# Idle TensorE turns, score vectors as rows, averages by chunk, and other due times in a two-layer graph kernel

## The chip, the cores and the metric

The kernel runs on one core of a Trainium2 chip. The metric is the device time of one execution in microseconds (us). TensorE (PE) multiplies and turns (transposes) tiles, VectorE (DVE), ScalarE (ACT) and GpSimd (POOL) work on elements, and SyncE (SP) issues most of the transfers; ACT and POOL issue the others. Each engine works through its own instructions in order and waits for others by semaphores.

## The reference

There are B = 32 graphs of N = 512 nodes with D = 128 features, and one adjacency matrix for all of them. Layer 0 is a graph attention, layer 1 a gated recurrence of five steps; both are added to their input.

```python
# layer 0
h = max(layernorm(x), 0) @ W
logits = leaky_relu(h @ a_src [:, None] + h @ a_dst [None, :], 0.2)
out = softmax(logits where adj > 0) @ h + b
x = x + leaky_relu(out, 0.3)
# layer 1, input h = max(layernorm(x), 0), five times:
m = adj @ h                      # in and out matrix are both adj
u3 = h @ u3_w.T + u3_b
z = sigmoid([m, m] @ w3_w.T + w3_b + u3)
r = sigmoid([m, m] @ w4_w.T + w4_b + u3)
hv = tanh([m, m] @ w5_w.T + w5_b + (r * h) @ u5_w.T + u5_b)
h = (1 - z) * h + z * hv
# result: x + h
```

## The kernel before, in words

Each graph is a tile of 128 partitions by K = 4 rows of 128 features. The program is not written in the order in which it runs. It adds tasks: each has an engine, its columns (from which `COST` gives a duration), a key (its due time, lower is earlier), what it needs, and the buffers or PSUM banks that it takes. `plan` (lines 69 to 121) then plays the engines forward: whichever engine can begin first takes the task with the lowest key among those that may begin about then. The tasks are issued in that order and `pin` keeps it. So a change of a key or of a price changes the order on every engine from there on, though no instruction.

What is done once, at the start: SP loads x of the first three graphs, the adjacency `a_sb` (1 MB), the weights and biases (`load_rest`); ACT's queue loads W (`gw`) and both score vectors, each spread over all 128 partitions (`across`, line 386). DVE multiplies `gw` with each (line 422), summing along the row, which gives `wa` = W a_src and W a_dst; ACT writes these beside W into `wrow` (430 to 433), so that one product `hp` (line 714) gives h and its scores. The adjacency is turned in blocks by TensorE (`at_ps`, line 449, four groups of four) and copied by ACT into `adjT` (457).

Layer 0 of a graph (`layer0`): layer norm (statistics at 570, 576, 577; the power on POOL at 582; for graph 0 centre and scale on DVE at 587 and 591, else ACT at 606); a turn of h (the first `DIRECT` = 4 graphs by TensorE, `t_a`, line 623; later ones by a DVE block transpose and transfers through DRAM on POOL's queue); the product hp; exponentials and scaling on ACT (`hw`, 720 and 725); the scores spread over partitions (`es`, line 739, four turns for the first four graphs, transfers after that); four weight tiles `pt` on DVE (784), one for each chunk c of 128 neighbours; and the average `av` on TensorE (809), two parts with two halves each, over all four chunks. DVE normalizes (819, 821), applies the leak (836), adds x (839), and a second layer norm gives hN, which is turned (`t_b`) into the state hT.

A step of `recurrence`: m from the two halves `hi` and `lo` of h (line 886, eight instructions), a copy mT (897), the gates g (905, 906, then 925), tanh on ACT (911, 932), rh on DVE (918), the candidate v (941, 942), its tanh (947), and three DVE operations (953, 959, 962) that update hT. Then h is turned back for the next step: for the first steps of the first `SHORT` graphs, and for the last step of the last `SHORT_END` = 3 graphs, by TensorE (`h`, line 977, four turns); otherwise by a DVE block transpose (990), one store and four loads on SP's queue (996, 1001). After the last step DVE adds x1 (1026) and SP stores the result (1031).

Due times: `due(b)` is 5 steps of 6100 ns for each graph, 3 in the last `LEVEL` = 8 graphs; a step of the recurrence is due `WIDTH` = 6 later than the one before; layer 0 begins `LEAD` = 11 steps ahead. In the last eight graphs the keys are capped so that all end together.

Of the kernel before, what the change touches and what calls it, by code (L numbers as in the profile page):

```python
# [10 lines left out]
F32 = mybir.dt.float32  # L11
F32R = mybir.dt.float32r
AF = mybir.ActivationFunctionType
ALU = mybir.AluOpType

P = 128
Q = 32
G = P // Q
STEPS = 5
# [3 lines left out]
PACE = 3  # L23
# [1 line left out]
SLOTS = 10  # L25
DIRECT = 4
SHORT = 3
SHORT_END = 3
LEVEL = 8
STEP = 6100  # L30
LEAD = 11
# [4 lines left out]
    "POOL": (650, 0, 130),  # L36
    "SP": (430, 0, 0),
}
LANDING = 2600

WAIT = {"DVE": 200, "ACT": 200}
# [231 lines left out]
def gat_then_gated_gnn_kernel(  # L273
# [20 lines left out]
    nc = tc.nc  # L294
    B, N, D = x.shape
    K = N // P
# [14 lines left out]
    pin = tc.keep_in_program_order  # L311
    tasks = []

    def add(*args, **kwargs):
        tasks.append(Task(*args, **kwargs))
        return tasks[-1]

    def new(buffer, name, shape=(P, N)):
        tag = buffer.tags[0]
        if "bank" in buffer.tags:  # L320
            buffer.tile = psum.tile([P, N], F32, tag="bank", name=name)
        elif tag in ("way", "turn", "line"):
            buffer.tile = dram.tile(list(shape), F32, tag=tag, name=name)
        else:
            buffer.tile = pools[BUFFERS[tag]].tile(list(shape), F32, tag=tag, name=name)
        return buffer.tile


    ident = const.tile([P, P], F32, name="ident")
    make_identity(nc, ident)  # L330
    ones = const.tile([P, P], F32, name="ones")
# [28 lines left out]
    prep = fast.enter_context(tc.tile_pool(name="prep", bufs=1))  # L360
    a_sb = prep.tile([P, K, N], F32, name="a_sb")
    gw = prep.tile([P, D], F32, name="gw")
    across = prep.tile([P, 2, D], F32, name="across")
    cols = prep.tile([P, 5], F32, name="cols")
    sums2 = prep.tile([P, 2], F32, name="sums2")
    half = const.tile([P, 2], F32, name="half")
# [16 lines left out]

    nc.scalar.dma_start(out=gw, in_=g_w)
    for i, v in enumerate((g_asrc, g_adst)):
        nc.scalar.dma_start(out=across[:, i, :], in_=v.partition_broadcast(P))

    def load_rest(name):
        if name == "a":
# [18 lines left out]
    bias_loaded = add("SP", [1] * 5, -9.4e9, lambda: load_rest("bias"), (rest_loaded,), lands=1000)  # L408


    soon = -100 * STEP

    def issue():
        pin(nc.gpsimd.tensor_copy(wrow[:, :D], gw))
        pin(nc.gpsimd.tensor_copy(wsrc[:, :D], gw))

    w_copied = add("POOL", [1], soon, issue, at=3600)
    products = prep.tile([P, 2, D], F32, name="products")

    def issue():  # L420
        for i in range(2):
            pin(nc.vector.scalar_tensor_tensor(
                products[:, i, :], gw, 1.0, across[:, i, :], ALU.mult, ALU.mult,
                accum_out=wa[:, i : i + 1],
            ))

    wa_made = add("DVE", [128] * 2, soon + 1, issue, at=5900)

    def issue():
        pin(nc.scalar.copy(wrow[:, D : D + 1], wa[:, 1:2]))  # L430
# [7 lines left out]
        at=60 * STEP)  # L438

    adjacency = []  # L440
# [32 lines left out]
    t = add("POOL", [1] * 3, 0, issue, (rest_loaded,))  # L473
# [9 lines left out]
    t = add("PE", [256] * 5, 0, issue, (t,), (f_ws, f_us))  # L483
# [56 lines left out]
    t = add("DVE", [1] * 4, late, issue, (*counted, wa_made))  # L540
# [7 lines left out]
    t = add("PE", [256], late, issue, (t,), (f_viol,))  # L548
# [117 lines left out]

    def due(b):

        early = B - LEVEL
        return 5 * b if b < early else 5 * early + PACE * (b - early)  # L670

    def layer0(b):
        direct = b < DIRECT
# [5 lines left out]
        def keys(i):  # L679
            return begin + length * (base[0] + i) / parts  # L680

        f_x, loaded = xs.pop(b) if b in xs else load_x(b)
        f_h, f_hT, f_hw = Buffer("h0"), Buffer("h0T"), Buffer("hw")
# [7 lines left out]
        t = relu_layernorm(h, lambda: f_x.tile, f"a{b}", keys, (loaded,), (f_x, f_h), b == 0)  # L691
        base[0] = 5
        turn = transposed if direct else blockwise
        t = turn(hT, h, f"a{b}", keys, (t,), (f_h, f_hT))
# [5 lines left out]
        def hw():  # L700
            return f_hw.tile or new(f_hw, f"hw_{b}", (P, K, D + 3))
# [31 lines left out]
        if direct:  # L733
# [9 lines left out]
            t = add("PE", [256] * K, keys(0), spread, made, (f_hw, f_es))  # L743
        else:
# [9 lines left out]
            t = add("DVE", [64], keys(0), gather, made, (f_hw, f_lines))  # L754
# [23 lines left out]
            t = add("POOL", [1], keys(2), spread, stores, (way, f_es), lands=LANDING + 1500)  # L778
        base[0] = 15
        f_pts = [Buffer(f"pt{c}") for c in range(K)]  # L780
# [11 lines left out]
        weighed = [weigh(c) for c in range(K)]  # L792
# [3 lines left out]
        def o():  # L796
            return f_o.tile or new(f_o, f"o_{b}", (P, K, D))

        def average(part):
            f = Buffer("o", "bank")  # L800

            def avs():
                return f.tile[:, : 2 * (D + 1)].rearrange("p (c e) -> p c e", c=2)

            def multiply():
                new(f, f"av_{b}_{part}")
                for i in range(2):
                    for c in range(K):
                        pin(nc.tensor.matmul(  # L809
                            avs()[:, i, :],  # L810
                            lhsT=f_pts[c].tile[:, ts(2 * part + i, P)],
                            rhs=hw()[:, c, : D + 1],
                            start=(c == 0),
                            stop=(c == K - 1),
                        ))

            def normalize():
                rsum = pools[3].tile([P, 2], F32, tag="rsum", name=f"rsum_{b}_{part}")
                pin(nc.vector.reciprocal(rsum, avs()[:, :, D]))
                for i in range(2):  # L820
                    pin(nc.vector.scalar_tensor_tensor(
                        o()[:, 2 * part + i, :], avs()[:, i, :D], rsum[:, i : i + 1], bias0,
                        ALU.mult, ALU.add,
                    ))

            u = add("PE", [4 * (D + 1)] * 2 * K, keys(part), multiply, weighed,
                    (f, f_hw, *f_pts))
            return add("DVE", [40, 180, 180], keys(1 + part), normalize, (u, rest_loaded),
                       (f, f_o))

# [36 lines left out]
    def recurrence(b, step, halved, turned):  # L867

        key = (due(b) + WIDTH * step) * STEP
        if b >= B - LEVEL:  # L870
            key = min(key, (5 * B - LEVEL * (STEPS - 1 - step)) * STEP)

        def keys(i):
            return key + i * STEP / 4
# [4 lines left out]
        def aggregate(which, first):  # L879
            part = (his if first else los)[b % SLOTS]  # L880

            def issue():
                if first:
                    new(f_m, f"m_{b}_{step}")
                for k in range(K):
                    pin(nc.tensor.matmul(  # L886
                        f_m.tile, lhsT=part[:, k, :], rhs=adjT[:, k, :],
                        start=(first and k == 0), stop=(not first and k == K - 1),
                    ))

            return issue

        high, low = halved
        t = add("PE", [512] * K, keys(0), aggregate("hi", True), (high, *adjacency), (f_m,))
        t = add("PE", [512] * K, keys(0), aggregate("lo", False), (t, low), (f_m,))
        t_m = add("ACT", [480], keys(1),
                  lambda: pin(nc.scalar.copy(new(f_mT, f"mT_{b}_{step}"), f_m.tile)), (t,),  # L897
                  (f_m, f_mT))
# [68 lines left out]

        last = step == STEPS - 1
        nth = 5 * b + WIDTH * step
        if nth < 5 * SHORT or (last and b >= B - SHORT_END):  # L970

            f = Buffer("o", "bank")

            def turn():
                h_ps = new(f, f"h_{b}_{step}")
                for k in range(K):
                    pin(nc.tensor.transpose(h_ps[:, ts(k, P)], hT[:, ts(k, P)], ident))

            needs = (add("PE", [256] * K, keys(6), turn, (turned,), (f,)),)
            view = ("p k d -> p k d", {})  # L980

            def src():
                return f.tile.rearrange("p (k d) -> p k d", k=K)
        else:


            f_b, way, f = Buffer("blocks"), Buffer("way"), Buffer("rows")

            def blocks():
                pin(nc.vector.transpose(  # L990
                    new(f_b, f"blocks_{b}_{step}").rearrange("p (g k q) -> p g k q", g=G, k=K),
                    hT.rearrange("p (k g q) -> p g k q", g=G, k=K),
                ))

            def store():
                pin(nc.sync.dma_start(out=new(way, f"way_{b}_{step}"), in_=f_b.tile))

            def load(g):
                def issue():
                    rows = f.tile or new(f, f"rows_{b}_{step}", (P, G, N // G))  # L1000
                    pin(nc.sync.dma_start(
                        out=rows[ts(g, Q)],
                        in_=way.tile.rearrange("(a q) (g e) -> g q a e", a=G, g=G)[g],
                    ))

                return issue

            t = add("DVE", [512], keys(6), blocks, (turned,), (f_b,))
            t = add("SP", [1], keys(6), store, (t,), (f_b, way), lands=LANDING)
            needs = []  # L1010
            for g in range(G):
                needs.append(add("SP", [1], keys(6), load(g), (t, *needs[-1:]), (way, f),
                                 lands=LANDING))
            view = ("p k (a q) -> p a k q", {"a": G})

            def src():
                return f.tile.rearrange("p a (k q) -> p a k q", k=K)
# [69 lines left out]
```

## Time and profile before

| | us |
|---|---|
| median of three runs | 1169.24 (1169.11 to 1169.42) |
| the profiled execution | 1170.99 |
| its span | 1169.2 |
| TensorE waits for the adjacency at the start | 8.2 |
| first aggregation m begins | 29.20 |
| last product v of the recurrence begins | 1158.99 |

The table's last three rows are from the list of waits and the timeline. The span is the time from the first to the last instruction of the profiled execution. In the lines that follow, a group of instructions is told by its start, its duration, engine, line, operation, and output <- inputs; the bracket at the end is how long the engine had been idle and who ended that. In tables of stretches each engine has its busy time and its number of instructions; the three last columns are the clock granted to TensorE, the busy share of the DMA engines, and GB/s. Matrix products are pipelined: the busy time of a product includes its passage through the array, so that the distance between the starts of two that follow each other is the price of one.

### The profile page before, as it was taken

The page shows a single profiled execution, that of the slowest core. Times are in us where ns is not written, and L with a number is a line of the kernel's source. Part 1 is how long each engine was busy: PE and PEld are TensorE (multiplying, and loading weights), DVE is VectorE, ACT ScalarE, POOL GpSimd, SP SyncE. Part 2 cuts the span into 40 slices and gives each one's busy share as a digit, 9 for nine tenths or more (in the row PEclk, how much of TensorE's full clock was granted, in tenths as well). Part 3 has the DMA queues.
Part 4 walks back from the last instruction along what each step waited for, and adds up shares of the span by engine and source line. Part 5 has one row for each costly group of instructions (what it writes and reads, how often), then busy time and mean ns, then how long its engine had stood idle before and what let it go on. Part 6 is the DMA issues. An engine that isn't in the chain of part 4 may idle for free.

```text
span 1169.2 us, 14964 instructions
## 1 busy us (share of the span) xinstructions
PE 1145.9 (98%) x4267; PEld 701.6 (60%) x4267; DVE 947.4 (81%) x2120; ACT 649.8 (56%) x1263; POOL 347.7 (30%) x499
## 2 busy tenths in 40 slices
PE   6999999999999999999999999999999999999997
PEld 5665656555656556656655656656666566555553
DVE  5877988778998778988788888968989887667665
ACT  5655656465565565555565555566465554545543
POOL 2224433243442143332423344314254421100000
PEclk9999999999999999999999999999999999999998
DMA  3013344444445444443544444433454433332332
GB/s 109 21 43 100 111 137 124 124 125 122 133 119 137 126 143 129 125 131 113 141 130 129 119 122 147 136 115 109 129 146 128 128 111 117 98 98 74 106 109 78
DMA packets 137655, 135.62 MB, mean 116 GB/s; under 512 B 22496, under 2 KB 100960, under 8 KB 137440
## 3 DMA queue, kind: packets, MB, share of 16 engines
q1 hardware_dynamic: 119664, 97.64, 26.5%
q0 software_dynamic: 17472, 36.79, 12.5%
q8 instruction: 35, 0.57, 0.2%
q14 instruction: 52, 0.43, 0.1%
q10 hardware_dynamic: 432, 0.20, 0.1%
HBM read 71.83 MB, written 62.71 MB: 115 GB/s over the span
## 4 chain that ended last, share of the span: by engine, by line
PE 84%; DVE 2%; DMA 1%; ACT 1%; issue 0%; POOL 0%; SPq 0%; DVEq 0%; POOLq 0%
PE m L886 22%; PE g L925 11%; PE v L942 11%; PE v L941 10%; PE g L905 10%; PE g L906 10%; PE av L809 8%; PE hp L714 2%; DMA rows<-way 1%; DMA es<-line 0%; DVE hT L962 0%; DVE d L953 0%; DVE d L959 0%; ACT hv L947 0%; DVE pt L784 0%; DMA line<-lines 0%
## 5 line engine op out<-in xcount | busy, mean ns | idle before, releaser
L886 PE MATMUL m<-adjT,hi 128*128 128x512 f32 x640 | 196.4, 438 | 0.0
L886 PE MATMUL m<-adjT,lo 128*128 128x512 f32 x640 | 194.9, 436 | 0.0
L911 ACT ACTIVATE rs<-g,zrb 128x512 f32<-128x512 f32 x160 | 109.7, 686 | 146.2 <-PE g L906 145.9
L947 ACT ACTIVATE hv<-v,vb 128x512 f32<-128x512 f32 x160 | 109.8, 686 | 106.6 <-PE v L942 106.0
L953 DVE TENSOR_TENSOR d<-hv,hT 128x512 f32<-128x512 f32 x160 | 108.9, 681 | 72.9 <-ACT hv L947 72.2
L925 PE MATMUL g<-mT,w3dT 128*128 128x512 f32 x320 | 163.4, 594 | 1.5 <-ACT rs L911 1.5
L942 PE MATMUL v<-rh,u5hT 128*128 128x512 f32 x320 | 163.5, 592 | 1.2 <-DVE rh L918 1.2
L906 PE MATMUL g<-mT,w4sT 128*128 128x512 f32 x320 | 163.5, 592 | 0.0
L905 PE MATMUL g<-hT,u3T 128*128 128x512 f32 x320 | 163.5, 592 | 0.0
L941 PE MATMUL v<-mT,w5sT 128*128 128x512 f32 x320 | 163.4, 592 | 0.0
L897 ACT COPY mT<-m 128x512 f32<-128x512 f32 x160 | 93.8, 586 | 121.1 <-PE m L886 120.8
L932 ACT ACTIVATE zs<-g,zrb 128x512 f32<-128x512 f32 x160 | 109.6, 685 | 78.5 <-PE g L925 77.3
L886 PEld LDWEIGHTS m<-adjT,hi 128*128 128x128 f32 x640 | 119.2, 188 | 53.6 <-issue 29.4
L886 PEld LDWEIGHTS m<-adjT,lo 128*128 128x128 f32 x640 | 119.0, 188 | 50.6 <-issue 28.6
L918 DVE SCALAR_TENSOR_TENSOR rh<-rs,hT 128x512 f32<-128x512 f32 x160 | 109.0, 682 | 48.1 <-ACT rs L911 47.5
L809 PEld LDWEIGHTS av<-hw,pt 128*128 128x128 f32 x1024 | 123.1, 191 | 14.5 <-issue 10.3
L809 PE MATMUL av<-hw,pt 128*128 128x129 f32 x1024 | 123.8, 275 | 0.2 <-DVE pt L784 0.2
L962 DVE SCALAR_TENSOR_TENSOR hT<-d,hT 128x512 f32<-128x512 f32 x160 | 110.6, 691 | 13.6 <-PE v L942 0.5
L990 DVE STREAM_TRANSPOSE blocks<-hT 128x512 f32<-128x512 f32 x151 | 106.4, 707 | 10.6 <-DMA way<-blocks 6.4
L959 DVE SCALAR_TENSOR_TENSOR d<-zs,d 128x512 f32<-128x512 f32 x160 | 110.3, 690 | 4.6
L645 POOL DMA_DIRECT2D turn_b<-blocks_b x112 | 74.2, 665 | 118.0 <-DVE blocks_b L635 111.0
L942 PEld LDWEIGHTS v<-rh,u5hT 128*128 128x128 f32 x320 | 60.7, 190 | 78.1 <-issue 62.9
(112 smaller groups left out, 1360.4 us busy)
## 6 DMA issues: line engine op xcount, KB each, us to landing
way<-blocks SPq DMA_DIRECT2D x151, 256.0 KB, 2.1
rows<-way SPq DMA_DIRECT2D x604, 64.0 KB, 2.0
x<-in_x_dram SPq DMA_DIRECT2D x32, 256.0 KB, 2.9
out_dram<-res SPq DMA_DIRECT2D x32, 256.0 KB, 2.2
turn_a<-blocks_a POOLq DMA_DIRECT2D x112, 64.0 KB, 2.2
h0T<-turn_a POOLq DMA_DIRECT2D x28, 256.0 KB, 3.8
es<-line POOLq DMA_DIRECT2D x28, 256.0 KB, 3.8
turn_b<-blocks_b POOLq DMA_DIRECT2D x112, 64.0 KB, 2.2
```

The source lines that it names most:

```text
L809: pin(nc.tensor.matmul(avs()[:, i, :], lhsT=f_pts[c].tile[:, ts(2 * part + i, P)], rhs=hw()[:, c, : D + 1], start=(c == 0), stop=(c == K - 1),
L886: pin(nc.tensor.matmul(f_m.tile, lhsT=part[:, k, :], rhs=adjT[:, k, :], start=(first and k == 0), stop=(not first and k == K - 1),))
L905: pin(nc.tensor.matmul(g, lhsT=u3T, rhs=hT, start=True, stop=False))
L906: pin(nc.tensor.matmul(g, lhsT=w4sT, rhs=f_mT.tile, start=False, stop=True))
L911: pin(nc.scalar.activation(new(f_r, f"rs_{b}_{step}"), f_g.tile, AF.Tanh, bias=rb, scale=0.5))
L925: pin(nc.tensor.matmul(f_g.tile, lhsT=w3dT, rhs=f_mT.tile, start=False, stop=True, skip_group_check=True))
L932: pin(nc.scalar.activation(new(f_z, f"zs_{b}_{step}"), f_g.tile, AF.Tanh, bias=zb, scale=0.5))
L941: pin(nc.tensor.matmul(v, lhsT=w5sT, rhs=f_mT.tile, start=True, stop=False))
L942: pin(nc.tensor.matmul(v, lhsT=u5hT, rhs=f_rh.tile, start=False, stop=True))
L947: pin(nc.scalar.activation(new(f_hv, f"hv_{b}_{step}"), f_v.tile, AF.Tanh, bias=vb))
L959: pin(nc.vector.scalar_tensor_tensor(d, f_z.tile, 1.0, d, ALU.add, ALU.mult))
L962: pin(nc.vector.scalar_tensor_tensor(hT, f_d.tile, 0.5, hT, ALU.mult, ALU.add))
```

## The change

- `idle`: 56 tasks with the last key of all (1e12) turn the identity on TensorE into a bank of their own. The first 26 may begin at 0.7 us of the plan's time and are priced at 480 columns, the other 30 from 8 us at 256; the planner puts them wherever it sees TensorE free.
- The score vectors are loaded as two rows on one partition (`avecs`), and one product with a row of ones (`as_ps`) spreads them over the partitions in PSUM, from which DVE reads them.
- In the first four graphs the averages are four tasks for each part, one for each chunk, each needing only its own pt.
- The first `EARLY` = 6 graphs are due 4 steps apart, not 5, so all later due times come 6 steps earlier; the cap in the last eight moves with them.
- An m product is priced at 527 columns in place of 512; the instruction is the same.
- `SHORT_END` = 4, and the last two steps, not the last alone, are turned by TensorE in these graphs.

```diff
-SHORT_END = 3
+SHORT_END = 4
+EARLY = 6
...
+FIRST_IDLE, IDLE = 26, 30
...
-    across = prep.tile([P, 2, D], F32, name="across")
+    avecs = prep.tile([1, 2, D], F32, name="avecs")
...
-        nc.scalar.dma_start(out=across[:, i, :], in_=v.partition_broadcast(P))
+        nc.scalar.dma_start(out=avecs[:, i, :], in_=v.rearrange("(o d) -> o d", o=1))
...
+    f_idle = Buffer("o", "bank")
+
+    def idle():
+        pin(nc.tensor.transpose((f_idle.tile or new(f_idle, "idle"))[:, :P], ident, ident))
+
+    for i in range(FIRST_IDLE + IDLE):
+        add("PE", [480 if i < FIRST_IDLE else 256], 1e12, idle, (), (f_idle,),
+            at=700 if i < FIRST_IDLE else 8000)
...
+    f_as = Buffer("o", "bank")
+
+    def issue():
+        pin(nc.tensor.matmul(
+            new(f_as, "as_ps")[:, : 2 * D], lhsT=ones[0:1, :],
+            rhs=avecs.rearrange("o i d -> o (i d)"), start=True, stop=True,
+        ))
+
+    t = add("PE", [1024], soon, issue, (), (f_as,), at=4100)
...
-                products[:, i, :], gw, 1.0, across[:, i, :], ALU.mult, ALU.mult,
+                products[:, i, :], gw, 1.0, f_as.tile[:, ts(i, D)], ALU.mult, ALU.mult,
...
-    wa_made = add("DVE", [128] * 2, soon + 1, issue, at=5900)
+    wa_made = add("DVE", [150] * 2, -5.6 * STEP, issue, (t,), (f_as,))
...
     def due(b):
-        early = B - LEVEL
-        return 5 * b if b < early else 5 * early + PACE * (b - early)
+        at = since = 0
+        for until, pace in ((EARLY, 4), (B - LEVEL, 5), (B, PACE)):
+            at += pace * max(0, min(b, until) - since)
+            since = until
+        return at
...
+            def product(i, c, start):
+                pin(nc.tensor.matmul(
+                    avs()[:, i, :],
+                    lhsT=f_pts[c].tile[:, ts(2 * part + i, P)],
+                    rhs=hw()[:, c, : D + 1],
+                    start=start,
+                    stop=(c == K - 1),
+                    skip_group_check=True,
+                ))
...
+            def multiply_with(c):
+
+                def issue():
+                    if c == 0:
+                        new(f, f"av_{b}_{part}")
+                    for i in range(2):
+                        product(i, c, c == 0 and i == 0)
+
+                return issue
...
-            u = add("PE", [4 * (D + 1)] * 2 * K, keys(part), multiply, weighed,
-                    (f, f_hw, *f_pts))
+            if direct:
+                u = None
+                for c in range(K):
+                    u = add("PE", [4 * (D + 1)] * 2, keys(part), multiply_with(c),
+                            (weighed[c], u), (f, f_hw, f_pts[c]))
+            else:
+                u = add("PE", [4 * (D + 1)] * 2 * K, keys(part), multiply, weighed,
+                        (f, f_hw, *f_pts))
...
-            key = min(key, (5 * B - LEVEL * (STEPS - 1 - step)) * STEP)
+            key = min(key, (5 * B - EARLY - LEVEL * (STEPS - 1 - step)) * STEP)
...
-        t = add("PE", [512] * K, keys(0), aggregate("hi", True), (high, *adjacency), (f_m,))
-        t = add("PE", [512] * K, keys(0), aggregate("lo", False), (t, low), (f_m,))
+        t = add("PE", [527] * K, keys(0), aggregate("hi", True), (high, *adjacency), (f_m,))
+        t = add("PE", [527] * K, keys(0), aggregate("lo", False), (t, low), (f_m,))
...
-        if nth < 5 * SHORT or (last and b >= B - SHORT_END):
+        if nth < 5 * SHORT or (step >= STEPS - 2 and b >= B - SHORT_END):
```

On TensorE the new order begins with 17 idle turns, the product that spreads the vectors, nine more idle turns and the first adjacency turns; 30 idle turns stand among the work of the first three graphs, nine of them ahead of the first averages.

More of the change, by code (lines that the diff above doesn't have):

```diff
@@ L797, in o @@
             return f_o.tile or new(f_o, f"o_{b}", (P, K, D))
+        f_avs = [Buffer("o", "bank") for _ in range(2)]
         def average(part):
-            f = Buffer("o", "bank")
+            f = f_avs[part]
             def avs():
                 return f.tile[:, : 2 * (D + 1)].rearrange("p (c e) -> p c e", c=2)
+            def product(i, c, start):
[7 more added lines that the diff above has]
+                ))
             def multiply():
@@ L808, in multiply @@
                     for c in range(K):
[L809 to L815, printed above, removed]
+                        product(i, c, c == 0)
+            def multiply_with(c):
[5 more added lines that the diff above has]
+                return issue
             def normalize():
```

## The prediction

> **What bounds the kernel.** I read busy time first, then the chain of waits, then PE's own waits, then the stretches.
>
> ```profile
> PE 1145.9 (98%) x4267; PEld 701.6 (60%) x4267; DVE 947.4 (81%) x2120; ACT 649.8 (56%) x1263; POOL 347.7 (30%) x499
> ...
> PE 84%; DVE 2%; DMA 1%; ACT 1%; issue 0%; POOL 0%; SPq 0%; DVEq 0%; POOLq 0%
> ```
>
> TensorE is the bound. The time is its work plus the time in which it has none, and only three things can change: work, idle, and work done slowly. Where is it idle?
>
> ```profile
> 0.00:8.20 8.20, 0.00 (x0) 0.02 (x1) 2.10 (x13) 1.49 (x2) 2.64 (x9) 1.00 0.68 217
> 8.20:16.60 8.40, 7.19 (x32) 6.55 (x32) 4.40 (x26) 5.33 (x17) 4.17 (x9) 1.00 0.44 132
> 16.60:28.50 11.90, 9.71 (x69) 7.86 (x69) 9.25 (x26) 7.45 (x26) 1.39 (x1) 1.00 0.10 24
> 28.50:44.50 16.00, 15.49 (x95) 11.94 (x95) 15.10 (x54) 6.50 (x12) 3.03 (x3) 1.00 0.06 17
> 44.50:110.00 65.50, 65.50 (x280) 42.52 (x279) 48.26 (x122) 41.93 (x90) 24.02 (x34) 1.00 0.20 56
> 110.00:160.00 50.00, 48.31 (x182) 28.97 (x181) 44.23 (x110) 29.85 (x62) 22.64 (x32) 1.00 0.43 126
> 160.00:1130.00 970.00, 969.77 (x3525) 587.91 (x3524) 801.90 (x1741) 543.06 (x1033) 289.83 (x411) 1.00 0.42 122
> 1130.00:1160.00 30.00, 28.83 (x87) 15.09 (x85) 19.42 (x29) 13.51 (x21) 0.00 (x0) 1.00 0.31 101
> 1160.00:1169.20 9.20, 1.12 (x5) 0.71 (x4) 2.77 (x4) 0.69 (x1) 0.00 (x0) 0.65 0.17 62
> ```
>
> (The first busy column is PE.) From 44.5 to 1130 only 1.92 us are idle, so no edit there can give more. The rest is the head (8.2 without any work, then half-empty until 28.5) and the tail (1.17 in the last 30 us, then 9.2 after the last matrix product). The head is also slow:
>
> ```profile
> 9.17 0.29 DVE L422 SCALAR_TENSOR_TENSOR products<-gw,across 128x128 f32<-128x128 f32 x1 [0.50 <-DMA across<-in_L_gnn_a_dst_dram]
> ...
> 10.13 1.11 PE L623 MATMUL t_a<-ident,h 128*128 128x128 f32 x4 [0.81 <-DVE h L591]
> ...
> 15.35 0.87 PE L739 MATMUL es<-ident,hw 128*128 128x128 f32 x4
> ...
> 16.34 2.73 DVE L784 SCALAR_TENSOR_TENSOR pt<-es,hw,adjT 128x512 f32<-128x512 f32 x4 [2.21 <-PE es L739]
> ...
> 16.62 1.48 PE L623 MATMUL t_a<-ident,h 128*128 128x128 f32 x4 [0.41 <-ACT h L606]
> ...
> 19.12 3.17 PE L809 MATMUL av<-hw,pt 128*128 128x129 f32 x26 [0.17 <-DVE pt L784]
> ```
>
> Turns that follow each other start 0.22 us apart until 16.2 (the first four take 1.10, one of them 0.43) and 0.11 apart later (at 22.12, 22.23, 22.34), although the granted clock column says 1.00 throughout. So PE ran at half speed until between 16.2 and 16.6.
>
> **The change, part by part.**
>
> *Idle turns and score rows.* 26 turns of the identity stand ahead of the first adjacency turns, 30 more in gaps of the first graphs. At 0.22 us the 26 cost 5.7 us, from 1.35 (the identity is ready at 1.32) to about 7.1; the adjacency lands at 8.2, which hides them. After the 17th stands the product that spreads the score vectors; it waits for their DMA, with nine turns, the adjacency turns and everything else on PE behind it. The broadcast loads landed 7.0 and 7.5 us after issue; a row of 0.5 KB (the bias columns) took 2.5, gw 3.3. Landing thus lies between 4.2 and 9.2; I take about 5, as the row is nearest to the small loads. The two products on DVE (0.29 + 0.08 each) then end near 6.8 instead of 9.47, and the scale of h at 7.5 instead of 10.08.
>
> Whether turns raise the clock is the question. The row: at 11.04 to 16.2 PE ran turns, eight hp products (1.95 us) and turns again, and was fast by 16.6 (the next av starts are 0.11 apart). [...] my sum below would be about -0.4 us; by the trace, where more than half of the work before the rise was turns, it is -3.1. The trace can't exclude that the hp products alone did it. I take the trace. [...] here fast running came 6.1 to 6.5 us after work began at 10.13[...]. The new stretch of work is some 6 us long, so the rise should be there by 8.2, but not surely.
>
> *The first graph, replayed* in the new order on each engine with the durations of the rows (turn 0.11, hp 0.11, copy 0.59, hw 0.85 per half, pt 0.68), old end to new end: h scaled 10.08 to 7.5; t_a 11.24 to 9.3 (it stands behind the first adjacency turns, so behind 8.2); h0T copied 11.87 to 10.0; hp 14.69 to 11.1; es 16.21 to 12.7; last pt 19.07 to 15.6 (DVE must be through with two layer norms by 12.8; in the old order that work ended at 14.13, and it follows the landing of x).
>
> *Averages chunk by chunk.* Before, 26 of 32 av instructions ran after the last pt was begun, ending at 22.29. Now those of a chunk run beneath the next pt; 32 x 0.11 from 13.55 end at 17.2. Normalized at 18.4 instead of 23.14; hN scaled at 23.4 instead of 28.49; the first aggregation starts at 24.1 instead of 29.20. So 5.1 us are gained on graph 0.
>
> *What is late next: DVE.* From 23.4 the new order puts layer norms of graphs 3 and 4, a block transpose and graph 2's pts ahead of graph 1's normalization. Adding its rows (12 big ones of 0.7, eight pts, norms) gives graph 1's hN on ACT at 43.5 to 45.1; before, it ran at 41.67. PE would wait some 1.3 us there. Comparing what PE has then done: at 45.75 the new order has, beyond what the old had at 44.47, one m (1.85), one pair of g (1.72), hp (0.90), es and t_a (0.44 each), 5.35 us. The old one reaches this at 49.82. **Head: -4.1 us** (-1 to -5.6).
>
> *First six closer, later keys.* No instruction is added; all due times move by six steps together, so only the order in the ramp and chance order later change. `527` columns alters the planner alone (its price for an m product becomes 0.230, the row shows 0.231 between starts). Idle time in the middle was 1.92 us; the new order may have anything from 0 to about 7 (one step with a single graph in flight: at the end of this trace 10.2 us pass from the second half of m at 1152.73 to hT at 1162.90, and with the first half 0.93, turns 0.6 and cast 0.65 a step takes 12.4, against 1.85 + 5 x 0.86 = 6.2 of work). I take 1.9, the nearest row: **0 us**.
>
> *Last turns by TensorE.* Groups of four turns rise from 9 to 14, so five more. Each is 0.44 us of PE on the path: **+2.2 us**. Removed are five block transposes (0.71, DVE idle beside PE) and 25 DMA issues on SP, which lay beside PE. What they cost was waits in the tail:
>
> ```profile
> 1137.27 1.13 PE L925 MATMUL g<-mT,w3dT 128*128 128x512 f32 x2 [0.78 <-ACT rs L911]
> ...
> 1156.77 0.66 PE L977 MATMUL h<-ident,hT 128*128 128x128 f32 x4 [0.39 <-DVE hT L962]
> ...
> 1162.96 1.11 PE L977 MATMUL h<-ident,hT 128*128 128x128 f32 x4 [2.95 <-DVE hT L962]
> ```
>
> In the new order the last two graphs run interleaved to the end; between a graph's last product of step 3 and its turn stand 3.7 us or more of other work, where 3.0 are needed. Both waits go: **-1.2 us** (0 to -1.2). After the last product the chain (tanh, three DVE operations, turns, sum, store) stays 9.2 us. The last turns may be fast (PE idles 2.1 instead of 2.95 before them: -0.5), and two stores come together (+0.5): 0.
>
> **Sum:** -4.1 + 0 + 2.2 - 1.2 = -3.1 us. The profiled execution took 1170.99 with a span of 1169.2; 1.8 lie outside. The runs' median is 1169.24, so the forecast is **1166.1** (the profiled one about 1167.9).
>
> **Rivals.**
> 1. *The turns don't raise the clock.* For: [...] no stretch of turns alone was seen to end fast. Against: the mix at 11 to 16. Idle turns between hp and es then cost 0.22 each, es ends at 16.4 as before, and only the chunks save (av end 20.4 against 22.29). Head about -1.4: -1.4 + 2.2 - 1.2 = -0.4, **1168.8**, no change.
> 2. *DVE is not late.* The planner may order the ramp better than my rows say: head -5.1, no idle in the middle (-1.9): -6.0, **1163.2**. For: 65 us without idle in the old ramp. Against: DVE was busy 15.1 of 16.0 us at 28.5 to 44.5.
> 3. *Slower: recurrences starve PE in the ramp.* With DVE late for the second and third graph, at 45 to 110 us only graph 0 has steps to run; each such step costs 12.4 - 6.2 = 6.2 us. One such step brings +3.1 and decides from 5.4 us of new idle on (over 0.2% slower); one and a half give 9.3 - 3.1 = +6.2, **1175.4**, one alone **1172.3**, which I take. For: DVE load in the ramp. Against: the old ramp had the same work and no wait after 44.5.
>
> **How the numbers follow.** What a measurement can tell from no change is 0.2%, 2.3 us. Forecast case 0.46 (1163.5 to 1168), rival 1 0.22, rival 2 0.20, rival 3 0.12. Faster by over 2.3 us: most of the forecast case (0.40), rival 2 whole, a little of rival 1 (0.04): 0.64. Slower: rival 3 and a little of rival 1: 0.12. The rest, 0.24, is the same. The range reaches from rival 2's better side to rival 1's worse: 1162.0 to 1170.2.
>
> **What would show it.** Right: adjacency turns 0.11 us apart at 8.2; products on DVE over by 7; first m near 24; no idle of PE at 1130 to 1160; 56 turns for line 977's successor. Wrong: turns still 0.22 apart at 10 us; score rows landing after 7; PE idle above 5 us between 40 and 200.

## The result, and the profile after

| | before | after |
|---|---|---|
| median of 20 runs | 1169.54 (1168.44 to 1171.47) | 1167.82 (1165.95 to 1170.98) |
| profiled execution, its span | 1170.99, 1169.2 | 1165.95, 1164.1 |
| first m begins | 29.20 | 24.53 |
| last v begins | 1158.99 | 1153.03 |

The ratio is 0.9984 (95% interval 0.9978 to 0.9991): 1.7 us faster, inside the 0.2% that the prediction called no change. In a second comparison the same kernel gave 0.9992 (0.9984 to 1.0000). The two profiles are further apart, 5.0 us: the one of before lies 1.5 us above its median, the one of after is the fastest of its 20 runs. And the runs of the change spread over 5.0 us, those of before over 3.0. Why, is the question of the experiments.

Busy time first, from the page of the changed kernel:

```profile
PE 1151.7 (99%) x4345; PEld 708.7 (61%) x4345; DVE 942.9 (81%) x2115; ACT 647.8 (56%) x1263; POOL 347.8 (30%) x499
```

PE has 5.8 us more to do (idle turns and the tail's turns) and yet less time passes. The stretches (columns as before):

```profile
0.00:8.20 8.20, 5.82 (x31) 5.12 (x32) 3.32 (x19) 1.96 (x6) 2.64 (x9) 1.00 0.76 288
8.20:16.60 8.40, 8.40 (x74) 8.20 (x74) 5.54 (x24) 7.00 (x19) 4.17 (x9) 1.00 0.22 49
16.60:28.50 11.90, 11.40 (x88) 10.29 (x87) 11.22 (x43) 6.73 (x22) 1.90 (x2) 1.00 0.08 23
...
44.50:110.00 65.50, 65.18 (x298) 43.72 (x297) 53.74 (x151) 42.30 (x93) 29.12 (x41) 1.00 0.24 66
110.00:160.00 50.00, 50.00 (x180) 30.13 (x179) 46.84 (x106) 29.58 (x58) 22.93 (x34) 1.00 0.47 135
160.00:1130.00 970.00, 969.59 (x3514) 586.07 (x3513) 791.22 (x1711) 538.93 (x1025) 281.72 (x399) 1.00 0.41 120
```

From 44.5 to 1130 PE is idle for 0.73 us in place of 1.92. The start in the timeline, and the first m:

```profile
1.38 3.89 PE L418 MATMUL idle<-ident 128*128 128x128 f32 x17 [1.38 <-POOL ident masks.py:199]
...
6.27 0.67 PE L435 MATMUL as_ps<-avecs,ones 1*128 1x256 f32 x2 [1.00 <-DMA avecs<-in_L_gnn_a_dst_dram]
...
6.87 1.21 PE L418 MATMUL idle<-ident 128*128 128x128 f32 x9
...
7.91 0.65 PE L471 MATMUL at_ps<-ident,a_sb 128*128 128x128 f32 x4
...
13.34 3.84 PE L833 MATMUL av<-hw,pt 128*128 128x129 f32 x32
...
24.53 1.16 PE L933 MATMUL m<-adjT,hi 128*128 128x512 f32 x4
```

Take the passage of the last one, 0.43 or 0.27 us, from the duration and divide by the number of steps: the first 17 turns are 0.22 us apart, the nine 0.12. So in this execution PE was fast by 6.3, within 5 us of its first turn, where before it was fast from about 16 on. All 32 av now run in one piece beneath the pts.

The score rows did something that the prediction's sum did not have: the adjacency, loaded at the same time, comes earlier. Its line before and after (KB, then us from issue to landing):

```profile
a_sb<-in_adj_dram SPq DMA_DIRECT2D x1, 1024.0 KB, 6.9
...
a_sb<-in_adj_dram SPq DMA_DIRECT2D x1, 1024.0 KB, 5.1
```

Issued at 1.2, it is there at 6.3 in place of 8.1. All three traces with broadcast loads (before, before_pace4, across) have 6.9, the eleven with rows 5.1 or 5.2. At the end:

```profile
1153.03 1.02 PE L989 MATMUL v<-rh,u5hT 128*128 128x512 f32 x2
1154.52 0.63 PE L1024 MATMUL h<-ident,hT 128*128 128x128 f32 x4 [0.47 <-DVE hT L1009]
1157.08 0.66 PE L1024 MATMUL h<-ident,hT 128*128 128x128 f32 x4 [1.93 <-DVE hT L1009]
```

There are no waits between 1125 and the last v, and the last turns take 0.66 in place of 1.11. But from the start of that v to the end 11.07 us pass, where it was 10.21: two stores of 256 KB, issued 1.17 us apart at most, land 3.8 us (median) after issue; the one at the end of the kernel before took 3.1.

**Where the 5.0 us between the profiles came from.** The last v begins 5.96 earlier: five more groups of turns +2.2, idle time in the middle -1.2, in the tail -1.2, so the head gave 5.96 + 2.2 - 1.2 - 1.2 = 5.8 (by subtraction; 4.7 of it show at the first m). The end gives 0.86 back.

### The profile page after: what moved, and what is told of

Read it like the earlier page. It is cut to its first block, busy times and chain, and to the rows that moved or that the text cites. A ratio compares the mean times of both kernels' runs of the same rounds, so it can differ in the third digit from the quotient of the medians.

```text
span 1164.1 us, 15045 instructions
## 1 busy us (share of the span) xinstructions
PE 1151.7 (99%) x4345; PEld 708.7 (61%) x4345; DVE 942.9 (81%) x2115; ACT 647.8 (56%) x1263; POOL 347.8 (30%) x499
## 3 DMA queue, kind: packets, MB, share of 16 engines
q1 hardware_dynamic: 116064, 95.02, 25.8%
## 5 line engine op out<-in xcount | busy, mean ns | idle before, releaser
L933 PE MATMUL m<-adjT,hi 128*128 128x512 f32 x640 | 199.1, 441 | 0.3 <-ACT hi L910 0.3
L604 POOL TENSOR_TENSOR rs_b<-ve_b,mhalf 128x4 f32<-128x4 f32 x32 | 36.1, 1127 | 266.6 <-DVE ve_b L599 184.7
L1037 DVE STREAM_TRANSPOSE blocks<-hT 128x512 f32<-128x512 f32 x146 | 102.8, 707 | 9.6 <-DMA way<-blocks 7.2
```

Source lines behind the costliest of these rows:

```text
L933: pin(nc.tensor.matmul(f_m.tile, lhsT=part[:, k, :], rhs=adjT[:, k, :], start=(first and k == 0), stop=(not first and k == K - 1),))
```

## The experiments

Every ratio is to the kernel before on the same chip, with its 95% interval. The runs are from several chips, on which the kernel before had medians of 1169.05 to 1169.98, so differences of medians below 1 us between chips say little.

| run | median us | ratio |
|---|---|---|
| after_again (the change once more) | 1168.48 | 0.9992 (0.9984 to 1.0000) |
| no_idle | 1168.92 | 0.9995 (0.9987 to 1.0003) |
| tail_undone | 1165.44 | 0.9975 (0.9966 to 0.9984) |
| pace5 | 1173.80 | 1.0045 (1.0032 to 1.0058) |
| steady23 | 1166.01 | 0.9970 (0.9958 to 0.9982) |
| steady_tail | 1164.17 | 0.9953 (0.9939 to 0.9967) |
| across | 1169.69 | 1.0001 (0.9993 to 1.0010) |
| no_chunks | 1170.91 | 1.0010 (1.0003 to 1.0017) |
| before_pace4 | 1173.41 | 1.0031 (1.0019 to 1.0043) |
| price512 | 1165.56 | 0.9961 (0.9947 to 0.9975) |
| steady_first | 1166.13 | 0.9966 (0.9954 to 0.9978) |
| steady_tail_again | 1164.56 | 0.9959 (0.9945 to 0.9973) |

### The change once more: where its runs differ

> The changed kernel once more, for a second trace and the spread of its runs. Before the profile of the change lay 1.9 us below its median and that of the kernel before 1.5 us above its own, so the two profiles (5.0 us apart) say more than the medians (1.7 us). Theory A (the clock rises at a different moment in each run): the runs spread over 4 to 5 us again, median about 1167.8, and this trace, if it is a slower run, shows turns 0.22 us apart after 7 us. Theory B (the spread is made by transfers or by the end of the kernel): turns are 0.11 apart from 7 us on here too, and a slower trace differs at another place.

The runs spread from 1166.82 to 1170.65, and the profiled one was the slowest, with a span of 1168.9. The same order, in the timeline of this run:

```profile
1.38 3.89 PE L418 MATMUL idle<-ident 128*128 128x128 f32 x17 [1.38 <-POOL ident masks.py:199]
6.38 1.19 PE L435 MATMUL as_ps<-avecs,ones 1*128 1x256 f32 x2 [1.11 <-DMA avecs<-in_L_gnn_a_dst_dram]
7.50 2.18 PE L418 MATMUL idle<-ident 128*128 128x128 f32 x9
9.47 1.06 PE L471 MATMUL at_ps<-ident,a_sb 128*128 128x128 f32 x4
...
12.87 1.06 PE L739 MATMUL hp<-wrow,h0T 128*128 128x131 f32 x8
```

Here the nine turns are 0.22 us apart and so are the adjacency turns; only hp at 12.87 is fast. And since the nine turns stand ahead of the adjacency in PE's order, they push its turns to 9.47, though the adjacency had landed at about 6.4 (5.2 us after issue). The first m begins at 27.5 in place of 24.5: 3.0 of the 4.8 us between the two spans. Another 1.2 is a single wait of an av for its pt at 947.5. Theory A holds for the larger part. Of the five traces with the change's start, three were fast by 6.3 (the change, tail_undone, pace5) and two only at about 11 and 13 (no_chunks, this one).

**What the traces record of the clock.** Every trace keeps a list of the moments at which the clock granted to TensorE changed to 1.0 or to 0.5. The clock column is made from this list and counts the time ahead of the first entry as 1.00; after that entry it can be read. With the broadcast loads (run `across`, below) it gives:

```profile
6.06:9.48 3.42, 1.39 (x10) 0.96 (x8) 0.52 (x5) 0.00 (x0) 0.54 (x1) 1.00 0.95 321
9.48:16.30 6.82, 6.08 (x29) 6.08 (x30) 3.61 (x23) 4.72 (x15) 4.17 (x9) 0.50 0.35 83
```

Between two recorded changes lie 3.413 and then 6.827 us in this trace, 13.653 and 3.413 in `steady_first`, 1146.878 in the profile of before and 1153.705 in that of the change: 1, 2, 4, 1, 336 and 338 times 3.413 us. The first rise does not come at the same moment in two traces of the same start: at 5.54 in the change, at 12.85 in after_again. The table takes the 3.413 us ahead of a recorded change and, counted back from there (in before_pace4 forward), other stretches of that length; it gives the share of each in which PE ran turns or products:

| run | stretch, us | share | clock afterwards |
|---|---|---|---|
| the change | 2.13 to 5.54 | 0.92 | rises |
| pace5 | 2.57 to 5.98 | 0.79 | rises |
| after_again | 2.61 to 6.02 | 0.78 | stays at half |
| after_again | 6.02 to 9.43 | 0.57 | stays at half |
| after_again | 9.43 to 12.85 | 1.00 | rises |
| no_chunks | 0.67 to 4.09 | 0.79 | stays at half |
| steady_first | 4.03 to 7.44 | 0.74 | stays at half |
| steady_first | 7.44 to 10.86 | 0.90 | rises |
| across | 2.65 to 6.06 | 1.00, turns alone | rises |
| across | 6.06 to 9.48 | 0.41 | falls |
| steady_first | 21.10 to 24.51 | 0.47 | falls |
| before_pace4 | 146.20 to 149.61 | 0.48 | stays full |

The product as_ps, of a single row, is left out of these shares. With it the stretches 6.02 to 9.43 of after_again and 4.03 to 7.44 of steady_first would have 0.90 and 1.00, and the clock did not rise at their ends. In the rows above a rise followed shares of 0.79, 0.90, 0.92 and 1.00, and none followed 0.57, 0.74, 0.78 and another 0.79; the full clock fell after 0.41 and 0.47 and stayed after 0.48. What holds between and beyond these shares was not shown. What differs between the runs is how the same turns lie to such a stretch: the 17 (1.38 to 5.27) fill 0.92 of the one that ends at 5.54 in the change, and 0.78 of the one that ends at 6.02 in after_again.

### Without the idle turns

```diff
     def idle():
-        pin(nc.tensor.transpose((f_idle.tile or new(f_idle, "idle"))[:, :P], ident, ident))
+        pass
```

> The changed kernel in the same order, with the 56 idle turns not issued. If they raise the clock early: the first 24 turns and hp products from 8 us on are 0.22 us apart again, es ends 2.6 us later, and the kernel takes about 2.5 us more than the change (about 1170.3). If the gain of the head comes from the score rows and the chunks alone: at most 0.5 us more than the change, or less than the change, since nothing stands in PE's way.

It took 0.4 us more than the change on the same chip, which is the rival's number; but neither theory was right. The trace:

```profile
7.42 1.13 PE L471 MATMUL at_ps<-ident,a_sb 128*128 128x128 f32 x4
8.70 1.11 PE L645 MATMUL t_a<-ident,h 128*128 128x128 f32 x4
9.60 1.92 PE L471 MATMUL at_ps<-ident,a_sb 128*128 128x128 f32 x8
11.31 1.28 PE L739 MATMUL hp<-wrow,h0T 128*128 128x131 f32 x8
```

Turns are slow until the rise at 11.75, es runs 1.1 us later (12.90 in place of 11.81) and the first m begins at 25.7. That is 1.2 later than with idle turns in a good start, and 1.8 earlier than with them in a bad one. So the idle turns, as the change places them, win and lose: about nothing on average.

### The wait for the score rows taken out of the middle

```diff
-FIRST_IDLE, IDLE = 26, 30
+FIRST_IDLE, IDLE = 23, 30
...
-    t = add("PE", [1024], soon, issue, (), (f_as,), at=4100)
+    t = add("PE", [1024], soon, issue, (), (f_as,), at=5500)
```

PE's order is now 23 idle turns, the product that waits for the score rows, the adjacency turns. The question is whether the pause between turns and product (5.27 to 6.27 in the change) makes the spread of the runs.

> The change with 23 idle turns and then the product that waits for the score rows, directly ahead of the adjacency turns (17, product, 9 in the change); the order on the other engines is that of the change. [...] PE is busy from 1.4 to about 6.6 and again from 6.3 at the latest, so all or nearly all runs are fast by 8 us and the first m begins by 25 in the trace; median 1 to 2 us below the change, near its fastest runs (1166 to 1167), spread 3 us or less. If the spread has another cause: median within 0.5 us of the change and a spread of 4 us again.

The runs lie between 1165.16 and 1167.62, and the median of 1166.01 is at the change's fastest runs. The start of this kernel in the timeline:

```profile
1.38 5.16 PE L418 MATMUL idle<-ident 128*128 128x128 f32 x23 [1.38 <-POOL ident masks.py:199]
6.47 0.69 PE L435 MATMUL as_ps<-avecs,ones 1*128 1x256 f32 x2
7.09 0.75 PE L471 MATMUL at_ps<-ident,a_sb 128*128 128x128 f32 x4
```

The product begins without a wait (no bracket), and the adjacency turns follow at once. The pause alone does not decide it: in the change and in pace5 the clock rose at 5.54 and 5.98 within a pause of 1.0 us, after shares of 0.92 and 0.79. The 23 turns reach to 6.54, where the 17 end at 5.27. Of the five traces with this start four rose at 5.3 to 7.2; in the fifth (steady_first, below) the turns filled 0.78 of the stretch from 0.62 to 4.03, the next held the product, and the clock rose at 10.86. There the first m began at 25.8, not at 27.5, since no idle turn stands between the landing of the adjacency and its turns, and of these 1.3 us 0.5 come from a second fall of the clock. Both count: a late rise should be rarer (four of five traces against three of five would not show it alone, the narrower spread of the runs fits), and it costs less.

### Score vectors over all partitions again

```diff
-    avecs = prep.tile([1, 2, D], F32, name="avecs")
+    across = prep.tile([P, 2, D], F32, name="across")
...
-        nc.scalar.dma_start(out=avecs[:, i, :], in_=v.rearrange("(o d) -> o d", o=1))
+        nc.scalar.dma_start(out=across[:, i, :], in_=v.partition_broadcast(P))
```

The product as_ps is left out, and the two on DVE read `across`.

> The change with the score vectors loaded over all partitions again, without the product; 26 idle turns in one piece. The products on DVE then wait for the broadcast loads until 8.3 and 9.2, hp cannot begin before wrow at about 9.9, and h is scaled at 10.1 rather than 8.1; the adjacency turns go first. If the score rows' gain is on the path: first m 1.5 to 2 us later than in a good start of the change (26 to 26.5), median 1168 or more. If the wait for the score rows costs as much as the rows bring (since it makes the clock late): median as the change or less, 1167 to 1168.

The median is 1169.69, 3.7 us above steady23 on the same chip and 1.2 to 1.9 above the change on others: the rows are worth much of the head. In this kernel's timeline, h is late (t_a waits until 10.22), and something else shows:

```profile
1.38 5.32 PE L418 MATMUL idle<-ident 128*128 128x128 f32 x26 [1.38 <-POOL ident masks.py:199]
8.12 0.75 PE L468 MATMUL at_ps<-ident,a_sb 128*128 128x128 f32 x4 [1.42 <-DMA a_sb<-in_adj_dram]
10.22 1.12 PE L642 MATMUL t_a<-ident,h 128*128 128x128 f32 x4 [1.36 <-DVE h L610]
11.13 1.91 PE L468 MATMUL at_ps<-ident,a_sb 128*128 128x128 f32 x8
```

26 turns in 5.32 us are 21 slow and 4 fast steps, and the record has the rise at 6.06: PE had run nothing but turns until then. The adjacency turns at 8.12 are fast. The gaps of 1.42 and 1.36 us leave PE busy for only 0.41 of the 3.413 us to 9.48, where the record has the fall; the turns at 10.22 are slow again (1.12 for four), and stay so until es at 16.41; the first m begins at 29.1. The prediction's reading of the rows' worth as 2.6 us of DVE time was too small: the first gap is there because the adjacency lands 1.8 us later beside broadcast loads, and with the two gaps came the fall at 9.48.

### Averages in one piece

```diff
-            if direct:
+            if False:
```

> The change with the averages of the first four graphs in one piece for each part, as before. If the chunks work as forecast: the first av ends 2 us later (26 of 32 instructions after the last pt), the first m 1.5 to 2 us later, median 1 to 2 us above the change. Rival (DVE and not PE sets the ramp after 24 us): within 0.5 us.

The median is 2.4 us above the second run of the change, and its fastest run (1168.51) is 1.7 to 2.6 above the change's fastest. This profile had a bad start (rise at 10.91, first m at 27.7), so the first m can't be compared as it is, but the way to it from es can: 13.73 us here (13.98 to 27.70) and 12.72 in both traces of the change (11.81 to 24.53, 14.79 to 27.51). By the traces the chunks are worth 1.0 us there, by the medians about 2; the rest, with an order that also changed, was not found.

### The tail as before

```diff
-SHORT_END = 4
+SHORT_END = 3
...
-        if nth < 5 * SHORT or (step >= STEPS - 2 and b >= B - SHORT_END):
+        if nth < 5 * SHORT or (last and b >= B - SHORT_END):
```

> The changed kernel with turns by TensorE only in the last step of the last three graphs, as before. By the prediction's sum (2.2 us of turns against 1.2 us of waits) plus the end that got 0.85 us longer in the profile of the change: 1 to 2 us faster than the change (1166 to 1166.8). Rival (the waits in the tail were worth more than the turns): 1 us slower than the change or more.

It was 3.0 us faster than the change on the same chip, more than expected. But eight of its eleven runs lie between 1164.57 and 1165.62, and its profile had a good start; its span, 1163.8, is only 0.3 below the change's. Part of the 3.0 was luck. So the same edit was made on the kernel with the steady start:

> The same with turns by TensorE only in the last step of the last three graphs, as before the change. If the tail edit costs (1.0 us of PE by the sum and some 0.85 at the end): 1 to 2.5 us faster than the run with 23 turns ahead (1164 to 1165.5). If the 3 us by which the kernel with the undone tail beat the change came from a lucky start in more of its runs: within 0.5 us of it.

1164.17 against 1166.01, 1.8 us: the new tail costs. The start of the last v says 0.8 (1152.23 against 1152.99), the spans 1.0, the medians of five and six runs 1.8, with intervals that overlap; 1.0 of PE and 0.85 at the end is what the sums give. The 0.85 is high: from the start of the last v 10.6 to 11.4 us pass in the seven traces with the new tail, and 10.5 to 10.7 in the five others with the new head, 0.4 less on average. This version is faster than both kernels, so it was run again:

> The version with 23 turns ahead and the tail as before once more, for a second trace and more runs. If it is the better version and not a lucky sample of five: ratio to the kernel before 0.994 to 0.9965 again, spread of its runs 3 us or less, where the change had 5. If not: above 0.997.

Ratio 0.9959, all runs between 1163.77 and 1165.53.

### The spacing of the first graphs, in both kernels

```diff
-EARLY = 6
+EARLY = 0
```

> The changed kernel with all graphs due 5 steps apart until the last eight, as before. If the spacing only reshuffles work under a busy TensorE: within 1 us of the change. Rival (the closer first six took away the 1.2 us of idle time at 110 to 160 us): 1 to 2 us slower than the change, with the idle time there again.

Both were wrong: it cost 5.3 us, and with a good start in its profile (first m at 24.5). PE's waits in the ramp, in the timeline of this run:

```profile
108.33 1.12 PE L972 MATMUL g<-mT,w3dT 128*128 128x512 f32 x2 [0.78 <-ACT rs L958]
...
112.71 2.11 PE L933 MATMUL m<-adjT,hi 128*128 128x512 f32 x8 [1.54 <-ACT hi L910]
...
117.70 1.20 PE L933 MATMUL m<-adjT,hi 128*128 128x512 f32 x4 [1.03 <-ACT hi L910]
```

At 112 and 117 PE waits for the next step of a recurrence. That is the kind of wait that the prediction's third rival described, here for the old spacing. From 44 to 800 PE is idle for 5.1 us where the change has about 0.6. Is closer spacing good in itself?

> The kernel before with the first six graphs due 4 steps apart and nothing else changed. Undoing the spacing in the changed kernel cost about 5 us. If closer graphs are worth that much in themselves (TensorE lacks work in the ramp at 5): 2 us or more faster than before, with less idle time of PE at 110 to 160 us. If it matters only together with the faster head, or the 5 us were a bad order that any other change of keys would also avoid: within 1.5 us of before, to either side.

The kernel before with nothing but `EARLY` became 3.4 us slower (1.0031). Idle time rose from 1.69 to 2.55 at 110 to 160 us, and from 1.17 to 2.82 at 1130 to 1160. So the spacing is not a gain of its own: it gained 5.3 us in one version and lost 3.4 in the other. That it fits the faster head, or that it is only the order that the planner happens to find, is argued and not shown.

This trace also says something of the kernel before. Its first 32 instructions on PE are those of before, but the clock rose at 13.08, where it rose at 15.88 in the profile of before, and es began at 14.33 in place of 15.35. So the kernel before has early and late starts too, and its profile was a late one.

### The planner's price, and the later idle turns

The next two start from steady_tail.

```diff
-        t = add("PE", [527] * K, keys(0), aggregate("hi", True), (high, *adjacency), (f_m,))
-        t = add("PE", [527] * K, keys(0), aggregate("lo", False), (t, low), (f_m,))
+        t = add("PE", [512] * K, keys(0), aggregate("hi", True), (high, *adjacency), (f_m,))
+        t = add("PE", [512] * K, keys(0), aggregate("lo", False), (t, low), (f_m,))
```

> The version with 23 turns ahead and the tail as before, with m priced at 512 columns instead of 527 in the planner (the instructions are the same, the order changes from the third graph on). By the prediction (the price moves nothing that the trace can show): within 0.7 us of that version (1163.5 to 1164.9). Rival (the planner's clock drifts away from the chip's by about 8 us over the kernel, so that transfers are planned too late or early): 1 us or more slower, with more waits of PE between 160 and 1130 us.

The median, 1165.56, lies above the 1163.5 to 1164.9 that I expected, on a chip on which the kernel before was 0.5 us slower as well. Ratio 0.9961 against 0.9953 and 0.9959: no difference that the intervals can tell.

```diff
-        add("PE", [480 if i < FIRST_IDLE else 256], 1e12, idle, (), (f_idle,),
+        add("PE", [480 if i < FIRST_IDLE else 256], 1e12,
+            idle if i < FIRST_IDLE else lambda: None, (), (f_idle,),
```

> The version with 23 turns ahead and the tail as before, with the 30 later idle turns planned but not issued; the order is otherwise the same. If PE, once fast, stays fast through the gaps of the ramp (some 1 us each): the same time within 0.4 us, or up to 0.5 faster since nothing stands in the way. If the gaps lower the clock again (as two gaps of 1.4 us within 3 us did in the run with the broadcast loads): turns 0.22 apart again after 12 us, the first m later than 25, and 1 us or more slower.

Ratio 0.9966; the profiled run was the slowest of six. In its timeline:

```profile
7.63 1.13 PE L472 MATMUL at_ps<-ident,a_sb 128*128 128x128 f32 x4
...
24.29 0.94 PE L646 MATMUL t_b<-ident,hN 128*128 128x128 f32 x4 [1.11 <-DVE hN L614]
25.03 1.15 PE L834 MATMUL av<-hw,pt 128*128 128x129 f32 x4
25.83 2.06 PE L934 MATMUL m<-adjT,hi 128*128 128x512 f32 x4
```

PE was slow until 10.86, then fast, and slow again from 24.51 to 27.92:

```profile
21.10:24.51 3.41, 1.60 (x12) 1.19 (x11) 3.25 (x15) 1.91 (x7) 1.39 (x1) 1.00 0.20 77
24.51:27.92 3.41, 3.41 (x14) 2.91 (x13) 3.41 (x8) 1.67 (x5) 0.00 (x0) 0.50 0.00 0
```

PE is busy for 1.60 of the 3.41 us of the first of these stretches, and the clock falls at its end: av and m take nearly twice their time (0.71 and 1.16 with the turns in place), and m lo begins at 28.2 rather than at 25.9. The first reading (fast once, fast for good) falls: here, without the later idle turns, the clock was lowered. They are not needed in every run: in no_idle, without them as well, the emptiest such stretch of the ramp (21.99 to 25.40) had 0.59, and the clock stayed.

## Why the prediction was right or wrong

The forecast was 1166.1 with a range that holds the 1167.82 measured; the direction was right. The size was not: 1.7 us in place of 3.1, within no change, while I gave faster by over 0.2% a chance of 0.64. That the median came so near is in part luck: the sum has no late starts, which cost up to 3 us in some of the runs, and it has 0 for the spacing, which was worth 5.3 us in this version.

- **The step that failed: "so the rise should be there by 8.2, but not surely".** The forecast was made for a start in which it is. In four traces with the same start it came at 5.54 (the change), 5.98 (pace5), 10.91 (no_chunks) and 12.85 (after_again): 3.0 us at the first m between two traces of the same kernel. I had priced 26 turns at 5.7 us and called them hidden by the adjacency's landing at 8.2. With the rows it lands at 6.3; in a bad start, the wait for the score rows and the nine turns behind it end at 9.5.
- **The profile taken for the median.** I set a span of 1169.2 beside a median of 1169.24. The profiled execution of before was itself a late one, 1.5 above the median of 20 runs, and its clock rose 2.8 us later than that of before_pace4. Profile against profile, the sum gives 1167.9 for what was 1165.95.
- **That turns raise the clock**: right. In the run with the broadcast loads PE did nothing but turns before the clock rose at 6.06, and in the change nothing but turns before 5.54. My reading of the trace before was late: the clock rose at 15.88, not at 16.2 to 16.6.
- **Score rows**: taken to land at about 5, landed at 6.27; the products ended at 7.5, not 6.8. In a good start it cost nothing: t_a ended at 9.0, forecast was 9.3.
- **The replayed head**: first m at 24.1 forecast, 24.53 measured in a good start. The chunks gained less than the 1.9 us of the first rival: from es to the end of the averages 5.4 us in place of 6.8 without them, and 1.0 at the first m.
- **DVE late, "PE would wait some 1.3 us there"**: 0.32 us. **Middle, 0 us**: -1.2. With these the head and middle gave 7.0 where the sum had 4.1; the second rival was near in the good start.
- **Last turns, +2.2 and -1.2**: as measured, with five groups of turns more and no wait left. **The end, 0**: the fast turns came (0.66; the clock fell at 1159.25, after them, while in steady23 it fell at 1156.69, ahead of turns at 1157.03), but the two stores cost more: +0.86 between the two profiles.
- **The spacing, "chance order"**: wrong to take 0: undoing it cost 5.3 us, doing it alone 3.4. That this is chance fits both, but is not shown.

What stays open: why the spacing suits one version and not the other, which is the largest single effect here, and why no rise followed the two stretches that the product of one row would fill to 0.90 and 1.00. Of the eleven traces with idle turns at the start, the clock rose 3.9 to 5.8 us after the first turn in eight, and 9.5 to 11.5 after it in three. In pace5's profile the last v begins 6.8 us later than in the change's; about 4.3 of them are idle time of PE, the rest was not found.

## What to carry to other kernels

Filler on TensorE is worth its place only if it can't stand in the way: put the instruction that waits behind all of it, and nothing but real work behind that. Here 23 turns ahead of the waiting product gave a median of 1166.01, 17 ahead and nine behind 1167.82 and 1168.48. Read from the traces how much filler it takes: after 23 turns the clock had risen by 7.2 in four of five traces, after 17 by 6.3 in three of five. And look at the work behind the filler: in steady_first PE was busy for 1.60 of 3.41 us, the clock fell, and the first four products of m took 2.06 us in place of 1.16. One profile is one execution: where a kernel's runs spread by more than the expected gain, a second trace of the same kernel tells more than another edit, and the place where two traces part is where to work. In a kernel ordered by a planner, compare an edit only with runs that keep the order, or make it on two versions: the spacing gained in one and lost in the other.

## What the hardware showed that was not expected

Up to the first change that a trace records, the clock column of the profile says 1.00 although turns run at half speed (0.22 us apart); there only the distance between starts shows it. The stretches between recorded changes were 3.413 us or a multiple of it, up to 1153.705 (338 times) in the change, and the first rise came at 5.54 in one trace of that kernel and at 12.85 in another. No long pause went ahead of a fall: gaps of 1.42 and 1.36 us (across), or of 0.70 and 1.11 (steady_first), stood where PE was busy for 0.41 and 0.47 of the last 3.413 us. A load of 1 MB landed 6.9 us after issue beside two broadcast loads of 64 KB each, and 5.1 beside the two rows. The second of these rows, 0.5 KB, was there 4.5 us after issue while the 1 MB was on the way; the bias columns of the same size, issued a little later, took 3.1 to 3.9 us in the change and 2.4 to 2.7 in before.
